# A graph layer's last two token blocks, computed as a fifth pair in seven products instead of eight

## The chip, the cores and the metric

The kernel runs on one core of one Trainium2 chip. The metric is the device time of one execution in microseconds (us); the time before is the median of three runs, 1125.27 us (1124.78 to 1126.44). The engines are named as in the profile: PE multiplies matrices (PEld is its loading of the stationary operand), DVE is the vector engine, ACT the scalar engine, POOL the GpSimd engine, and SP only issues DMAs here.

## The reference

`x` holds 1250 tokens (graph nodes) of width D = 1024; `src` and `dst` name 40000 edges. Two graph layers with a residual, then a mixture of eight experts with a residual:

```python
def _sage_layer(h, edge_src, edge_dst, deg_inv, W_self, W_neigh, b):
    msg = h[edge_src]
    agg = jax.ops.segment_sum(msg, edge_dst, num_segments=h.shape[0])
    mean = agg * deg_inv[:, None]
    return h @ W_self + mean @ W_neigh + b
...
deg_inv = 1.0 / jnp.maximum(deg, 1.0)
h = jax.nn.relu(_sage_layer(x, edge_src, edge_dst, deg_inv, W_self0, W_neigh0, b0))
out = _sage_layer(h, edge_src, edge_dst, deg_inv, W_self1, W_neigh1, b1)
...
x = x + _L0_gnn_ref(_layernorm(x, axis=-1), src, dst, ...)
x = x + _L0_ffn_ref(_layernorm(x, axis=-1)[None], ...)[0]
```

All is float32. `_L0_ffn_ref` routes each token to two of eight experts by a two-layer router (`rw1`, `rw2`) and adds their weighted outputs.

## The kernel before

**Blocks.** The tokens lie in NB = 10 blocks of P = 128; block 9 has 98. `hT1` holds the first layer's output transposed: 8 slices of 128 features (KD = 8) by 1250 tokens. `C` holds, for every pair of blocks, how often each source is joined to each target, so a sum over edges is a product with `C`.

**First layer.** It goes by four quarters q of the columns: products of the tokens with `w_neigh0` (`y_unit`, L514), then products with `C` (L550), whose sums DVE multiplies by `dinv` (1/degree along the free axis, made at q = 0, L543 and L544), adds to `hT1` (L557, L558), and ACT passes through a relu (L559). Temporary rows lie in `tmp`, a stretch of the scratch area `SC`.

**Second layer.** It works in column halves of 512, four in all: two of `w_neigh1` (`y_half`, each followed by `sum_half`, the product with `C`) and two of `w_self1` (`own_half`). Within a half, blocks 0 to 7 are taken as four pairs (j, 4+j) by `two_blocks`. The two blocks (as columns B), the two halves of the features and the two column quarters of the weights (A) make a product of two 2x2 block matrices, and it is done in seven block products of KB = 4 matmuls instead of eight (the Strassen-Winograd scheme). For that, DVE makes sums of tokens once (`T1`, `T2`, `T4` in `ts`, and `T3` over the second half's tokens in `hT1`) and sums of weights in every half (`S1` to `S4`, `weight_sums`). The order of the products on PE is A11, S2, A12, S3, S1, A22, S4 (L628); ACT copies the first to `u2` (L636), DVE adds further products to `u2` and `u3`, and `store` hands on four quarters of rows. Each of `u2`, `u3` and the `spare` rows of `store` lies in a ring in `SC`. Blocks 8 and 9, which no pair holds, are multiplied plainly by `plain_rows`: 8 matmuls of 512 columns each (L615).

**Where the plain blocks stand.** They come first in both `y_half` calls and in `own_half` 0, and last in `own_half` 1. `y_half` splits every result into a high and a low part (`zh` by ACT at L382, `zl` by DVE at L383). `sum_half` loads `x` for a block into a ring of six buffers `xs` in `SC` (L693, SP's queue), POOL adds `b1` (L694), PE multiplies `C` with `zh` and `zl` (L698), DVE multiplies by `dinv_p` (1/degree by partition) and adds (L702), and SP stores the rows to `v_d` (L703). `dinv_p` is made by 20 DVE instructions at the head of the second layer (L607, L608), from `dinv`.

**Own halves and the end.** `xa` is loaded from `v_d` (L724), and `own_half` adds the products to it: DVE where a quarter is ready in PSUM (L140, the line of the helper `tt` that records every DVE tensor operation), POOL otherwise (L744). The weight sums of the last half are made between the two own halves. In the last half `finish` runs for each finished block: layernorm on DVE (L319 to L326, a root on ACT at L323), a store to `t_d`, POOL's `xa += t` (L340), the store to `out` (L341); two blocks later `turn_back` transposes the normalised rows on PE (L774) and ACT copies them into `hT1` (L778). Then the router begins: its `token_sums` on DVE write `xw`, which lies over `xa`, so they wait for the last store from `xa`; PE meanwhile has other products (L1174, L1188, L1127).

**Order.** The order of instructions on each engine is set when the program is built, by a scheduler that takes what its model says is ready; on the chip each engine goes strictly in that order, and so does each DMA queue. PSUM tiles go round in pools: `mm` (3 tiles, name `ps`), `mmb` (3, name `psb`), `tpp` (2, name `tp`, for transposes).

Of the kernel before, what the change touches and what calls it, by code (L numbers as in the profile page):

```python
# [10 lines left out]
F32 = mybir.dt.float32  # L11
# [3 lines left out]
I32 = mybir.dt.int32  # L15
# [6 lines left out]
P = 128  # L22
# [7 lines left out]
def kernel(  # L30
# [165 lines left out]
    nc.scalar.dma_start(out=b0_p, in_=b0.rearrange("(k p) -> p k", p=P))  # L196


    ext = const.tile([R, 3, 2], F32, name="ext")
    base_i = const.tile([1, NGR], I32, name="base_i")  # L200

    keys = const.tile([GP, 2, 2 * GC, R], F32, name="keys")
    worst = const.tile([1, 1], F32, name="worst")
    plain = const.tile([1, 1], I32, name="plain")
    gx = L[:1, 8000 : 8000 + 3 * NGR].rearrange("o (a g) -> o a g", a=3)
# [138 lines left out]
    def gnn_windows():  # L344
# [28 lines left out]

        yh = yp.tile([P, NB, QW], F32R, name="yh")
        yl = yp.tile([P, NB, QW], F32R, name="yl")
        win = yp.tile([P, NB * WIN], F16, name="win")
        win_i = yp.tile([P, NB * WIN], I32, name="win_i")
        nc.gpsimd.iota(win_i, pattern=[[1, NB * WIN]], base=0, channel_multiplier=0)
# [143 lines left out]
        for q in range(4):  # L522
            w_q = w_next
            w_next = load_q(w_neigh0, q + 1) if q < 3 else None
            for b in range(NB):
                if q == 0:
                    some_groups(1)
                y_unit(w_q, h0T, b, yh[: rows[b], b, :], yl[: rows[b], b, :])
            if q == 3:
                w_half = load_half(w_neigh1, 0)  # L530
            if q == 0:
                some_groups(R)
                while open_rows:
                    close_row()

                for c0, n in cchunks:
                    ps = mm.tile([P, 512], F32, name="ps")
                    for k in range(NB):
                        nc.tensor.matmul(
                            ps[:, :n], ones_r, C[:, k, c0 : c0 + n],  # L540
                            start=(k == 0), stop=(k == NB - 1),
                        )
                    nc.vector.tensor_scalar(dinv[:, c0 : c0 + n], ps[:, :n], 1.0, None, op0=ALU.max)  # L543
                    nc.vector.reciprocal(dinv[:, c0 : c0 + n], dinv[:, c0 : c0 + n])  # L544
            for c0, n in cchunks:
                for d in (2 * q, 2 * q + 1):
                    ps = mm.tile([P, 512], F32, name="ps")
                    for k in range(NB):
                        for part in (yh, yl):
                            nc.tensor.matmul(  # L550
                                ps[:, :n], part[: rows[k], k, (d % 2) * P : (d % 2 + 1) * P],
                                C[: rows[k], k, c0 : c0 + n],
                                start=(k == 0 and part is yh), stop=(k == NB - 1 and part is yl),
                            )
                    t = tmp[:, n_tmp % 4, :n]
                    n_tmp += 1
                    nc.vector.tensor_tensor(t, ps[:, :n], dinv[:, c0 : c0 + n], ALU.mult)  # L557
                    nc.vector.tensor_tensor(t, t, hT1[:, d, c0 : c0 + n], ALU.add)  # L558
                    nc.scalar.activation(hT1[:, d, c0 : c0 + n], t, AF.Relu)  # L559
        y0.close()  # L560


# [37 lines left out]
                tt(B12[:, i, :], B22[:, i, :], B12[:, i, :], ALU.subtract)  # L600
        T3 = B12

        dinv_p = small.tile([P, NB], F32, name="dinv_p")
        for b in range(NB):
            m = rows[b]
            d_t = tmp[:, b % 4, :P]
            nc.vector.tensor_tensor(d_t[:m, :m], dinv[:m, blk(b)], ident[:m, :m], ALU.mult)  # L607
            nc.vector.tensor_reduce(dinv_p[:m, b : b + 1], d_t[:m, :m], AX.X, ALU.add)  # L608
        nc.sync.dma_start(out=row_of(3), in_=bcast(b1, D))

        def plain_rows(w, b):
            m = rows[b]
            ps = mm.tile([P, 512], F32, name="ps")
            for k in range(KD):
                nc.tensor.matmul(  # L615
                    ps[:m], hT1[:, k, blk(b)], w[:, k, :], start=(k == 0), stop=(k == KD - 1)
                )
            return ps[:m]

        def two_blocks(ws, j, u, store):  # L620

            A11, A12, A22, S1, S2, S3, S4 = ws
            b, b2 = j, NA + j
            js = slice(j * P, (j + 1) * P)

            def product(ps, rows_of, w, first):
                for k in range(KB):
                    nc.tensor.matmul(  # L628
                        ps, rows_of(k), w[:, k, :], start=(first and k == 0),
                        stop=(k == KB - 1), skip_group_check=not first,  # L630
                    )

            u2, u3 = u[:, 0, :], u[:, 1, :]
            pa = mm.tile([P, 512], F32, name="ps")[:, :QW]
            product(pa, lambda k: hT1[:, k, blk(b)], A11, True)
            nc.scalar.copy(u2, pa)  # L636
            pb = mm.tile([P, 512], F32, name="ps")[:, :QW]
            product(pb, lambda k: T2[:, k, js], S2, True)
            tt(u2, u2, pb, ALU.add)
            product(pa, lambda k: hT1[:, KB + k, blk(b)], A12, False)  # L640
            store(b, 0, pa, None)
            pc = mmb.tile([P, 512], F32, name="psb")[:, :QW]
            product(pc, lambda k: T3[:, k, js], S3, True)
            tt(u3, u2, pc, ALU.add)
            pd = mmb.tile([P, 512], F32, name="psb")[:, :QW]
            product(pd, lambda k: T1[:, k, js], S1, True)
            store(b2, 1, pd, u3)
            product(pc, lambda k: T4[:, k, js], A22, False)
            store(b, 1, pc, u2)
            product(pd, lambda k: hT1[:, KB + k, blk(b2)], S4, False)  # L650
            store(b2, 0, pd, u2)

        def ring(v, n):
            v = v.rearrange("p (a n) -> p a n", n=QW)
# [7 lines left out]

        us, _ = ring(SC[:, :1024], 4)
        _, spare = ring(SC[:, 1024:2048], 4)
        xs = SC[:, : 3 * D].rearrange("p (a n) -> p a n", n=HALF)
        b1_r = row_of(3)

        with tc.tile_pool(name="y1", bufs=1, side="right") as y1:
            yh = y1.tile([P, NB, HALF], F32R, name="zh")
            yl = y1.tile([P, NB, HALF], F32R, name="zl")  # L670

            def y_half(ws):
                for b in range(2 * NA, NB):
                    split(yh[: rows[b], b, :], yl[: rows[b], b, :], plain_rows(w_half, b))

                def store(b, c, ps, u):
                    if u is not None:
                        t = spare()
                        tt(t, u, ps, ALU.add)
                        ps = t  # L680
                    cs = slice(c * QW, (c + 1) * QW)
                    split(yh[:, b, cs], yl[:, b, cs], ps)

                for j in range(NA):
                    two_blocks(ws, j, us[:, 2 * (j % 2) : 2 * (j % 2) + 2, :], store)

            def sum_half(h):

                hs = slice(h * HALF, (h + 1) * HALF)
                for b in range(NB):  # L690
                    m = rows[b]
                    v = xs[:m, 5 - b % 6, :]
                    nc.sync.dma_start(out=v, in_=x[blk(b), hs])  # L693
                    nc.gpsimd.tensor_tensor(v, v, b1_r[:m, hs], ALU.add)  # L694
                    ps = mm.tile([P, 512], F32, name="ps")
# [6 lines left out]
                    stt(v, ps[:m], dinv_p[:m, b : b + 1], v, op0=ALU.mult, op1=ALU.add)  # L702
                    nc.sync.dma_start(out=v_d[blk(b), hs], in_=v)  # L703

            y_half(ws)
            w_half = load_half(w_neigh1, 1)
            sum_half(0)
            ws = weight_sums(w_half, S_first)
            y_half(ws)
            w_half = load_half(w_self1, 0)  # L710
            sum_half(1)
            ws = weight_sums(w_half, S_first)
# [3 lines left out]
        own = st.enter_context(tc.tile_pool(name="own", bufs=1, side="right"))  # L716
        xa = own.tile([P, NB, D], F32, name="xa")
        more = own.tile([P, 2 * WQ + 4 * KB * QW + 2048], F32, name="more")
        alone = list(range(2 * NA, NB))
        paired = [b for j in range(NA) for b in (j, NA + j)]  # L720
        for h, order in enumerate((alone + paired, paired + alone)):
            hs = slice(h * HALF, (h + 1) * HALF)
            for b in order:
                nc.sync.dma_start(out=xa[: rows[b], b, hs], in_=v_d[blk(b), hs])  # L724
# [3 lines left out]
        _, spare = ring(more[:, -1024:], 4)  # L728

        def own_half(w, ws, h, done):  # L730
            def rows_alone():
                for b in alone:
                    v = xa[: rows[b], b, h * HALF : (h + 1) * HALF]
                    tt(v, v, plain_rows(w, b), ALU.add)
                    done(b)

            def store(b, c, ps, u):
                v = xa[:, b, h * HALF + c * QW : h * HALF + (c + 1) * QW]
                if u is None:
                    tt(v, v, ps, ALU.add)  # L740
                else:
                    t = spare()
                    tt(t, u, ps, ALU.add)
                    nc.gpsimd.tensor_tensor(v, v, t, ALU.add)  # L744

            if h == 0:
                rows_alone()
            for j in range(NA):
                two_blocks(ws, j, us[:, 2 * (j % 2) : 2 * (j % 2) + 2, :], store)
                done(j)  # L750
                done(NA + j)
            if h == 1:
                rows_alone()

        n_done = [0]

        def finish(b):
            t = row_of(n_done[0] % 4)
            n_done[0] += 1
            after_layers(b, xa, t)  # L760
            turned.append((b, t))
# [5 lines left out]
        def turn_back():  # L767
# [3 lines left out]
            for q in range(0, KD, 4):  # L771
# [5 lines left out]
                for i in range(4):  # L777
                    nc.scalar.copy(hT1[:, q + i, blk(b)], ps[:, i, :m])  # L778

        own_half(w_half, ws, 0, lambda b: None)  # L780
        ws = weight_sums(w_last, more[:, 2 * WQ : -2048])
        turn[0] = 0
        route_w.append(load_pair(rw1, 0))
        route_w.append(load_pair(rw1, 1))
        own_half(w_last, ws, 1, finish)
        while turned:
            turn_back()
        st.close()
# [919 lines left out]
```

## Time and profile before

| what | us |
|---|---|
| median of the three runs | 1125.27 |
| time of the profiled execution | 1124.47 |
| span of its profile | 1122.5 |
| PE busy | 1090.3 |
| plain blocks of one half, L615 (433.41 to 447.15) | 13.74 |
| one pair of one half, 7 products, L628 (447.15 to 459.23) | 12.08 |
| `sum_half`, L698 (495.66 to 542.11 on the chain) | 46.45 |
| the ten sums for `dinv_p`, L607 and L608, each mean | 0.287 and 0.284 |

The profile is of one execution; times in it count from the start of its span. A float32 matmul of the program shows as two MATMUL records. "Busy" of PE is modelled, since matmuls are pipelined: the distance between the starts of two records is the better measure, and the table's stage times are such distances.

### The profile page before, as it was taken

What the parts mean: (1) busy time and instruction counts of PE and PEld (TensorE: products, weight loads), DVE (VectorE), ACT (ScalarE), POOL (GpSimd) and SP (SyncE); (2) the same over time, 40 slices, a digit from 0 to 9 for tenths busy, and PEclk for the clock granted to TensorE, in tenths of its full rate; (3) what the DMA queues carried; (4) which work ended last, traced back from release to release, by engine and by line L of the source; (5) the groups of instructions that cost most, each with busy time, mean ns of one, the idle gap of its engine ahead of it and who ended that gap; (6) DMA issues with size and microseconds to landing.
All of it is one profiled execution on the core that took longest, in us unless ns stands there. A gap on an engine that the chain in (4) does not pass through costs nothing.

```text
span 1122.5 us, 13221 instructions
## 1 busy us (share of the span) xinstructions
PE 1090.3 (97%) x4729; PEld 786.5 (70%) x4729; DVE 466.2 (42%) x1145; ACT 185.3 (17%) x418; POOL 334.6 (30%) x441
## 2 busy tenths in 40 slices
PE   6999999999999999999999999999999999999994
PEld 5555556888888886888688868886544487676762
DVE  8777777762121236233134122364522173222221
ACT  4301000001111111110011000022211134232321
POOL 2899999900000000013002202254000013332321
PEclk9999999999999999999999999999999999999997
DMA  7011011010100021032103270334870456767763
GB/s 239 31 38 40 1 38 39 1 38 1 38 1 1 1 75 38 1 125 98 36 1 131 92 273 3 90 158 166 313 240 1 149 184 171 185 181 194 194 169 51
DMA packets 62317, 107.33 MB, mean 96 GB/s; under 512 B 8906, under 2 KB 35690, under 8 KB 62240
## 3 DMA queue, kind: packets, MB, share of 16 engines
q1 hardware_dynamic: 51392, 79.69, 20.8%
q0 software_dynamic: 7056, 23.88, 9.1%
q10 hardware_dynamic: 3792, 2.79, 0.8%
q8 instruction: 42, 0.69, 0.3%
q14 instruction: 35, 0.29, 0.1%
HBM read 80.74 MB, written 27.42 MB: 96 GB/s over the span
## 4 chain that ended last, share of the span: by engine, by line
PE 91%; DMA 3%; POOL 2%; DVE 2%; issue 1%; ACT 0%; SPq 0%; DVEq 0%; POOLq 0%
PE ps L514 12%; PE ps L451 11%; PE psb L628 10%; PE ps L698 8%; PE ps L550 8%; PE ps L628 7%; PE ps L1519 6%; PE ps L1546 6%; PE ps L1174 5%; PE ps L615 5%; PE ps L1188 4%; PE cnt L412 3%; DMA out_dram<-L 2%; PE ps L1127 2%; POOL ol L402 1%; PE tp L1502 1%
## 5 line engine op out<-in xcount | busy, mean ns | idle before, releaser
L402 POOL TENSOR_SCALAR ol<-lane,keys 125x128 f16<-125x128 f16 x320 | 192.8, 621 | 23.6 <-DVE oh L409 23.6
L451 PE MATMUL ps<-h0T,L 128*128 128x498 f32 (+2 forms) x384 | 147.9, 517 | 0.6 <-DMA L<-in_L_gnn_W_self_dram 0.4
L694 POOL TENSOR_TENSOR L<-L 128x512 f32<-128x512 f32 (+1 forms) x20 | 31.7, 1595 | 374.0 <-DMA L<-in_L_gnn_b_dram 215.3
L514 PE MATMUL ps<-L,h0T 128*128 128x256 f32 (+1 forms) x640 | 142.0, 379 | 0.0
L514 PEld LDWEIGHTS ps<-L,h0T 128*128 128x128 f32 (+1 forms) x640 | 118.4, 188 | 17.9 <-issue 0.5
L409 DVE TENSOR_SCALAR oh<-win,keys 125x240 f16<-125x240 f16 x320 | 83.6, 315 | 32.0 <-PE cnt L412 29.8
L451 PEld LDWEIGHTS ps<-h0T,L 128*128 128x128 f32 x384 | 67.5, 191 | 38.5 <-issue 34.0
L1519 PE MATMUL ps<-xw,L 128*128 x368 | 84.1, 380 | 0.7 <-issue 0.7
L1546 PE MATMUL ps<-xw,L 128*128 x184 | 82.8, 593 | 0.5 <-ACT L L1534 0.5
L550 PE MATMUL ps<-C,yh 128*128 128x256 f32 (+2 forms) x240 | 81.8, 356 | 0.0
L550 PE MATMUL ps<-C,yl 128*128 128x256 f32 (+2 forms) x240 | 81.5, 353 | 0.0
L698 PE MATMUL ps<-zh,C 128*128 128x512 f32 (+1 forms) x200 | 79.5, 398 | 0.0
L698 PE MATMUL ps<-zl,C 128*128 128x512 f32 (+1 forms) x200 | 78.6, 393 | 0.0
L1519 PEld LDWEIGHTS ps<-xw,L 128*128 128x128 f32 x368 | 68.0, 190 | 9.6 <-issue 1.4
L1552 POOL DMA_INDIRECT out_dram<-L x23 | 36.5, 1586 | 118.4 <-DVE L L1551 85.7
L431 DVE TENSOR_TENSOR C<-C,cnt 128x240 f32 x160 | 64.3, 402 | 11.7 <-DVE C L431 1.0
L1491 POOL DMA_INDIRECT L<-t_d,L x26 | 25.5, 979 | 143.9 <-DVE L L140 123.1
L1546 PEld LDWEIGHTS ps<-xw,L 128*128 128x128 f32 x184 | 34.9, 190 | 34.9 <-issue 32.3
L412 PEld LDWEIGHTS <-ol 125*128 125x128 f16 x320 | 31.0, 97 | 37.0 <-POOL ol L402 22.1
L1551 DVE SCALAR_TENSOR_TENSOR L<-ps,L 128x512 f32<-128x512 f32 x46 | 34.5, 751 | 53.1 <-PE ps L1546 53.1
L383 DVE TENSOR_TENSOR yl<-ps,yh 128x256 fp32r<-128x256 f32 (+1 forms) x40 | 16.9, 424 | 92.5 <-ACT yh L382 92.5
L140 DVE TENSOR_TENSOR L<-L,ps 128x512 f32<-128x512 f32 (+1 forms) x28 | 17.1, 611 | 86.7 <-PE ps L1174 44.5
(223 smaller groups left out, 1523.4 us busy)
## 6 DMA issues: line engine op xcount, KB each, us to landing
xw<-in_L_ffn_ew_dram SPq DMA_DIRECT2D x16, 1024.0 KB, 10.6
L<-in_L_ffn_eb_dram SPq DMA_DIRECT2D x23, 512.0 KB, 4.0
L<-in_x_dram SPq DMA_DIRECT2D x20, 256.0 KB, 2.8
v_d<-L SPq DMA_DIRECT2D x18, 256.0 KB, 2.0
xa<-v_d SPq DMA_DIRECT2D x18, 256.0 KB, 6.2
t_d<-L SPq DMA_DIRECT2D x9, 512.0 KB, 3.2
out_dram<-xa SPq DMA_DIRECT2D x9, 512.0 KB, 2.7
L<-in_L_gnn_W_self_dram SPq DMA_DIRECT2D x4, 1024.0 KB, 5.5
```

The lines of the kernel that those rows point to most:

```text
L402: nc.gpsimd.tensor_scalar(ol[:, c, :], lane[:GP], keys[:, 1, c, r : r + 1], None, op0=ALU.is_equal)
L409: nc.vector.tensor_scalar(oh, win[:GP], keys[:, 0, i * GC + c, r : r + 1], None, op0=ALU.is_equal)
L412: nc.tensor.matmul(ps[:, i, :GW], ol[:, i * GC + c, :], oh, start=(c == 0), stop=(c == GC - 1),)
L431: nc.vector.tensor_tensor(to, to.bitcast(F32), ps[:, i, :GW].rearrange("p (k w) -> p k w", k=NB), ALU.add,)
L451: nc.tensor.matmul(ps[:, :n], w[:, k, (d % 2) * P : (d % 2 + 1) * P], h0T[:, k, c0 : c0 + n], start=(k == 0), stop=(k == KD - 1),)
L514: nc.tensor.matmul(ps[:m, :QW], hT[:, k, blk(b)], w[:, k, :], start=(k == 0), stop=(k == KD - 1))
L550: nc.tensor.matmul(ps[:, :n], part[: rows[k], k, (d % 2) * P : (d % 2 + 1) * P], C[: rows[k], k, c0 : c0 + n], start=(k == 0 and part is y ...
L615: nc.tensor.matmul(ps[:m], hT1[:, k, blk(b)], w[:, k, :], start=(k == 0), stop=(k == KD - 1))
L628: nc.tensor.matmul(ps, rows_of(k), w[:, k, :], start=(first and k == 0), stop=(k == KB - 1), skip_group_check=not first,)
L698: nc.tensor.matmul(ps[:m], C[: rows[k], k, blk(b)], part[: rows[k], k, :], start=(k == 0 and part is yh), stop=(k == NB - 1 and part is yl),)
L1519: nc.tensor.matmul(ps[:, :H], xT[:, k, :], w1_all[:, ds(e, 1), k * H : (k + 1) * H], start=(k == 0), stop=(k == KD - 1),)
L1546: nc.tensor.matmul(ps, hT[:, q, :], w2_all[:, ds(e, 1), q * D + h * HALF : q * D + (h + 1) * HALF], start=(q == 0), stop=(q == KH - 1),)
```

## The change

In the second layer, blocks 8 and 9 become a fifth pair of `two_blocks` in all four halves, and `plain_rows` is gone. Their token sums `Te1`, `Te3` lie in a new tile `te`, `Te2`, `Te4` in `SC` (elements 2048 to 3071), made once by `last_sums`: five DVE instructions and one ACT copy. Since block 9 has 98 rows, its products have 98 output rows, the last rows of `u3` are copied from `u2` by ACT, and the A22 product goes to a PSUM tile of its own (`pe`).

What goes with it: the first two pairs of `y_half` 0 start with their A11 and A12 products (`amid`), ahead of all that use the token sums. `dinv_p` is made in the first layer at q = 0. The ring `xs` has four buffers, which lie over the rings of `u2`, `u3` and `spare`. `xa` is loaded in the order of the pairs, blocks 8 and 9 last. The last half's weight sums are made inside `own_half` 0, after its second pair. `finish` uses three row buffers in turn, not four. `ext`, `base_i` and `keys` move to the pool of the first layer.

```diff
+            if q == 0:
+                dinv_p = small.tile([P, NB], F32, name="dinv_p")
+                for b in range(NB):
+                    m = rows[b]
+                    d_t = tmp[:, b % 4, :P]
+                    nc.vector.tensor_tensor(d_t[:m, :m], dinv[:m, blk(b)], ident[:m, :m], ALU.mult)
+                    nc.vector.tensor_reduce(dinv_p[:m, b : b + 1], d_t[:m, :m], AX.X, ALU.add)
...
+        def last_sums():
+            B11, B21 = hT1[:, :KB, blk(b8)], hT1[:, KB:, blk(b8)]
+            B12, B22 = hT1[:, :KB, blk(b9)], hT1[:, KB:, blk(b9)]
+            tt(Te1, B12, B11[:, :, :M2], ALU.subtract)
+            tt(Te2[:, :, :M2], B22, Te1, ALU.subtract)
+            nc.scalar.copy(Te2[:, :, M2:], B11[:, :, M2:])
+            tt(Te4, B21, Te2, ALU.subtract)
+            tt(Te3, B22, B12, ALU.subtract)
...
-        def plain_rows(w, b):
-            m = rows[b]
-            ps = mm.tile([P, 512], F32, name="ps")
-            for k in range(KD):
-                nc.tensor.matmul(
-                    ps[:m], hT1[:, k, blk(b)], w[:, k, :], start=(k == 0), stop=(k == KD - 1)
-                )
-            return ps[:m]
...
             product(pa, lambda k: hT1[:, k, blk(b)], A11, True)
             nc.scalar.copy(u2, pa)
+            yield
+            if amid:
+                product(pa, lambda k: hT1[:, KB + k, blk(b)], A12, False)
+                store(b, 0, pa, None)
+                yield
...
+            product(pc[:m2], lambda k: t3[:, k, :], S3, True)
+            if m2 < P:
+                past = slice(m2 // LQ * LQ, P)
+                nc.scalar.copy(u3[past], u2[past])
+            tt(u3[:m2], u2[:m2], pc[:m2], ALU.add)
...
+            if m2 == P:
+                product(pc, lambda k: t4[:, k, :], A22, False)
+                store(b, 1, pc, u2)
+            else:
+                pe = mmb.tile([P, 512], F32, name="psb")[:, :QW]
+                product(pe, lambda k: t4[:, k, :], A22, True)
+                store(b, 1, pe, u3)
...
-            def y_half(ws):
-                for b in range(2 * NA, NB):
-                    split(yh[: rows[b], b, :], yl[: rows[b], b, :], plain_rows(w_half, b))
...
+                if h == 0:
+                    two = [pair(j, True) for j in range(2)]
+                    for _ in range(2):
+                        for p in two:
+                            next(p)
+                    for p in two:
+                        list(p)
+                for j in range(0 if h else 2, NA + 1):
+                    list(pair(j))
...
-                    v = xs[:m, 5 - b % 6, :]
+                    v = xs[:m, 3 - b % 4, :]
...
+            for j in range(NA + 1):
+                list(two_blocks(ws, j, us[:, 2 * (j % 2) : 2 * (j % 2) + 2, :], store))
+                if h == 0 and j == 1:
+                    ws_last.extend(weight_sums(w_last, more[:, 2 * WQ : -2048]))
+                for b in (j, NA + j) if j < NA else (b8, b9):
+                    done(b)
...
-            t = row_of(n_done[0] % 4)
+            t = row_of((0, 1, 3)[n_done[0] % 3])
```

## The prediction

> **What bounds the kernel now.** I read the page's first, second and fourth part, then the groups by line and shape, then the timeline at the places where the change puts an edge. First the page:
>
> ```profile
> PE 1090.3 (97%) x4729; PEld 786.5 (70%) x4729; DVE 466.2 (42%) x1145; ACT 185.3 (17%) x418; POOL 334.6 (30%) x441
> ...
> PE   6999999999999999999999999999999999999994
> ...
> PEclk9999999999999999999999999999999999999997
> ...
> PE 91%; DMA 3%; POOL 2%; DVE 2%; issue 1%; ACT 0%; SPq 0%; DVEq 0%; POOLq 0%
> ```
>
> PE is busy in every slice at an undivided clock, and the chain that ended last runs through PE for 91%. From 433 to 782 us, the second layer, no other engine stands on the chain. So what PE saves there comes off the end, unless a new wait takes it. The groups by line and shape, L615 the plain blocks and L628 the products of pairs:
>
> ```profile
> L615 PE MATMUL ps<-L 128*128 128x512 f32 x48 | 21.1, 592 | 0.0
> L615 PE MATMUL ps<-L 128*98 128x512 f32 x48 | 21.1, 592 | 0.0
> ...
> L628 PE MATMUL ps<-L 128*128 128x256 f32 x192 | 45.4, 379 | 0.0
> ```
>
> The reader sees no idle time ahead of either, and that 98 output rows cost as much as 128: the moving columns set the time. Distances of starts, from the timeline of PE:
>
> ```profile
> 433.41 13.90 PE L615 MATMUL ps<-L 128*128 128x512 f32 x32
> 447.15 1.89 PE L628 MATMUL ps<-L 128*128 128x256 f32 x8
> 448.87 1.89 PE L628 MATMUL ps<-ts 128*128 128x256 f32 x8
> ...
> 459.23 1.89 PE L628 MATMUL ps<-L 128*128 128x256 f32 x8
> ```
>
> Last, the edge from the layer to the router, all engines; E below is the end of the last half's products, 781.96 here:
>
> ```profile
> 781.96 1.04 PE L774 MATMUL tp<-ident,L 128*128 128x128 f32 x8
> 782.60 1.45 ACT L778 COPY L<-tp 128x128 f32<-128x128 f32 x8 [6.11 <-PE tp L774]
> 783.86 0.37 ACT L323 ACTIVATE rs<-mv,eps 98x1 f32<-98x1 f32 x1
> 784.51 1.45 ACT L778 COPY L<-tp 128x128 f32<-128x128 f32 x8 [0.28 <-PE tp L774]
> 785.35 2.37 POOL L340 TENSOR_TENSOR xa<-xa,L 98x1024 f32<-98x1024 f32 x1 [5.39 <-DVE L L326]
> 787.75 0.35 SPq L341 DMA_DIRECT2D out_dram<-xa  x1
> 788.15 0.92 PE L1127 MATMUL ps<-L 128*128 128x226 f32 x4
> 791.00 2.89 DVE L140 TENSOR_TENSOR xw<-L 128x2048 f32<-128x2048 f32 x2 [5.74 <-DMA out_dram<-xa]
> 798.00 2.31 PE L1174 MATMUL ps<-xw 128*128 128x512 f32 x5
> ```
>
> Here block 9's finish, its store and the router's token sums run beside PE's transposes and first products. The sums (T2 and S2, done by 796.7) are in time for 798.00 with 1.3 us to spare.
>
> **Part 1, the products.** Removed in each half: 2 blocks, 32 records, 447.15 - 433.41 = 13.74 us. Added: 7 products of 8 records, 459.23 - 447.15 = 12.08 us; the 98-row ones count the same by the two L615 rows. Saved: 1.66 us a half, 6.64 us in four halves. All of it lies on the path.
>
> The row of 256 columns (12.08/56 = 215.7 ns a record) costs half of the row of 512 (13.74/32 = 429.4 ns). The Trainium skill, in "TensorE: Matmul & The Clock Gate", section "Back-to-back issue gap", adds a fixed 2.5 ns to every stream of columns, and "Perfetto Trace Analysis", section "Matmuls", says that "Larger matmuls are more efficient than smaller matmuls, when possible"; both speak against cutting 512 into 256. By the page, at two streams of 109.2 and 215.8 ns to a record, an estimate, the saving would be 4 x (13.81 - 12.23) = 6.3 us. The rows show no such penalty.
>
> **Part 2, the end of the last half.** Before, blocks 8 and 9 finished 7.7 us apart (774.22 and 781.96), with PE at work in between. Now both finish at E, as blocks 1 and 5 do at 751.05, and that end gives the rows. There the sixth product ends at 749.32; DVE adds at 749.52, POOL at 750.03, statistics run at 750.78. So block 8's statistics stand at E - 0.3, its root on ACT at E + 0.7, its normalising (L326, 1.25) to E + 2.6; block 9's statistics (0.69) and aggregate (0.21) to E + 3.4, root to E + 3.75, normalising to E + 5.5 (1.64, the L326 row beside POOL's L340 at 769.83).
>
> The order of the changed program on ACT is: root of 8, copies of block 3, root of 9, copies of 7 and 8, copies of 9. Before, the copies of 7 stood ahead of the last root. Eight copies take 1.45 us and `tp` has two tiles. So PE goes: transposes of 3 (E to 0.87), one router matmul (0.86), transposes of 7 behind the copies of 3 (to E + 3.0), one matmul (3.85); ACT is held at the root of 9 until E + 3.75, so 8's transposes run 4.6 to 5.7, a matmul to 6.6, 9's to 7.45, a matmul to 8.3. Then L1127. Before it stood at 788.15 - 781.96 = E + 6.2; with the transposes of block 3 (0.87), formerly ahead of E, 7.06 is work, and 8.3 - 7.06 = 1.24 us is new waiting. Transposes of 2 and 6 now fall among half-long matmuls, as at 736.76 to 740.69: 0.2 us more. Given back: 1.44 us. Bounds: nothing, if ACT's order does not bind; 3.6 if the last store from `xa` lands after 6.6 us (the slowest of the ten first `xa` loads) and not 3.15 (787.75 to 790.90). With 3.15, T2 and S2 come at E + 5.5 + 2.4 (L340) + 3.2 + 5.7 (791.00 to 796.7) = E + 16.8, and PE asks at 8.3 + 9.85 (788.15 to 798.00) = E + 18.15. With 6.6 PE waits 2.2 more. I take 1.44, since its rows are of the same operations.
>
> **Edits costed at nothing.**
> - `dinv_p`: 20 DVE instructions, 5.7 us, leave 426 to 440 us, where DVE had the slack, and enter the first quarter's L550 (238 to 261 us on PE). There DVE does 1.36 us of work for each 4.5 us of PE and idles some 3.1 us before every unit, so 2 to 3 sums (1.7 us) fit; without that cover the next splits would start up to 1.7 us late, under three PSUM tiles. No DMA moves with them.
> - Head of the layer: pairs 0 and 1 start with four products that need no sums (6.9 us, to 440.3). T2's last part ended about 436.9 and T4 at 438.7, both behind the last relu (435.65). `last_sums` stands behind them: about 0.56 x 4 (392 columns, between 0.42 at 256 and 0.69 at 512) + 0.69 = 2.9 us, to about 441.9 with a split between, and the first addition to `u2` is asked for at 442.0. A cover lost would cost that difference once.
> - `xs` of four, the queues: the first `x` of `sum_half` now waits for the last split, 1.6 us into it, and is issued behind the half's 2 MB of weights. The issue at 495.31 behind such weights took 7.3 us. SP's order still puts the weights ahead of it, at the row's 493.96. On DVE the sums S1 and S3 now stand ahead of the eviction of block 0 (L702), so that eviction waits for the weights: 502.0 + 3.46 + 0.75 = 506.2, 10.7 us into the stage; PE asks for that PSUM tile after three blocks, 3 x 4.65 = 13.9. Slack 3.2 us. At the other end of the rows, 12.1 us to land (the weights of the last half), PE waits 0.85 us in each of two halves: 0 to 1.7. A gain is excluded, since L698 has no idle before it.
> - `xa` in the order of pairs: DVE adds block 0 at 5.2 us into `own_half` 0, not at 18.9. The first load of that queue landed in 3.3 us, the slowest of ten in 6.6. If it took 10.5 (the slowest of twenty), DVE's `u3` would hold up the A22 product by about 3.1 us; else 0.
> - Sums of the last weights: same four instructions (1.22 each) inside a pair that comes after 668.1, where the weights landed; three row buffers: each is rewritten after its transposes in PE's order; POOL's extra adds (0.72 each) and ACT's copies of 32 rows end within a product.
>
> **Sum.** -6.64 + 1.44 = -5.20 us. The profiled execution, 1124.47 (span 1122.5), becomes 1119.27; it stood 0.80 under the median, so the median becomes 1120.1.
>
> **The rivals.**
> - A: the ACT order costs nothing, because the scheduler's gaps fall otherwise on the chip: -6.64, 1118.6. For it: at the earlier pair ends (736.76, 751.05) PE waited only 0.24 us for ACT. Against: two finishes at once.
> - B: the last store from `xa` decides, 2.2 us more: 1122.3. For it: the 5.74 us wait of DVE at 791.00 ends on that store. Against: slack 1.3.
> - C, mild and strong: the weights ahead of the eviction, at 12.1 us to land, 1.7 us more: 1121.8. It is also the case of the other side: the place is block 3 of `sum_half`, the price is 2 us per us of landing beyond 11.2, and from 14.9 us on the kernel is slower than before: 7.4 us of waiting eat the 5.2 and the bound of measurement, 1127.5. For it: the slowest expert load took 14.8. Against: such weights landed in 8.1 us at 502.0 and in 7.9 at 610.4.
> - D: the late `xa`, 3.1 us: 1123.2, no change. Against: block 0 is first in the queue.
>
> **How the numbers follow.** 0.2% (2.25 us) is about what a measurement of this kernel tells from no change. Chances: forecast 0.60, A 0.15, B 0.07, C mild 0.06, C strong 0.06, D 0.06. Faster holds all but D and strong C: 0.88; same 0.06; slower 0.06. The range takes in A with the spread of the runs below the median (0.5) and B: 1118.0 to 1122.4, leaving out D and strong C.
>
> **What would show it.** Right: no L615; L628 distances of 215 to 216 ns also where the form is 128*98; pairs of 12.1 us, five to a half; `sum_half` at 46.4 us with no idle; 6 to 9 us from the last product to L1127, with transposes waiting for L778. Wrong: PE waiting for L702 in `sum_half` (C), for `u3` in the first own pair (D), at the first product with `xw` (B), or products of the fifth pair that take longer than the others.

## The result and the profile after

The changed kernel takes 1122.63 us (median of 7 runs, 1120.86 to 1123.13), the kernel beside it 1125.85 (7 runs): a ratio of 0.9974, 95% interval 0.9965 to 0.9983, about 2.9 us faster. The forecast was 5.2 us faster; the sign was right, the size was not, and 1122.6 lies just outside the range. The profiled execution took 1122.76 us (span 1120.8), against 1124.47 (1122.5) before.

The page of the changed kernel, parts 1, 2 and 4 (busy time, PE's clock by slices, the chain that ended last):

```profile
PE 1084.8 (97%) x4825; PEld 803.8 (72%) x4825; DVE 473.7 (42%) x1171; ACT 189.2 (17%) x431; POOL 335.9 (30%) x447
...
PEclk9999999999999999999999999999999999999997
...
PE 75%; DMA 14%; DVE 4%; issue 4%; POOL 1%; ACT 1%; SPq 0%; POOLq 0%; DVEq 0%; ACTq 0%
```

PE is busy for 5.5 us less (before: 1090.3), and the span is only 1.7 us shorter: part of what was saved is idle now. Of the chain's 14% of DMA, 12% lies behind 942 us, in the experts' stores to `out`, which end beside PE's last products; an experiment below with the unchanged second layer shows the same 12% there. Whether a run's chain is followed through them says nothing about this change. Another 1% is the load of the last weights, which matters below.

PE's groups by line and form (L648 is the line of the pairs' products now; then busy time, mean ns of one, idle time before them and its cause):

```profile
L648 PE MATMUL ps<-L 128*128 128x256 f32 x240 | 56.2, 379 | 0.0
L648 PE MATMUL psb<-ts,L 128*128 128x256 f32 x192 | 45.5, 380 | 0.6 <-DVE more L140 0.6
L648 PE MATMUL psb<-L,ts 128*128 128x256 f32 x96 | 22.8, 380 | 0.6 <-DVE more L140 0.6
...
L648 PE MATMUL psb<-ts,te 128*98 128x256 f32 x48 | 10.8, 379 | 0.0
```

The plain blocks are gone, the 98-row products of the fifth pair cost the same 379 ns of modelled time, and two groups have idle time that no group of the pairs had before. PE's waits from 434 to 803 us, the second layer and the head of the router, say where (total, times, longest):

```profile
PE psb L648 <- DVE more L140: 1.2, 2, 0.6
PE ps L1214 <- DVE L L140: 0.9, 1, 0.9
PE tp L814 <- ACT L L818: 0.7, 3, 0.2
PE ps L1214 <- ACT L L818: 0.2, 1, 0.2
```

In the kernel before, the same view has one line, 0.5 us for ACT's copies. The waits for DVE, two in the pairs and one in the router's head, are new.

The stages, as distances of starts on PE (us; "half" is the first product of a column half to the first product after it):

| | before | after |
|---|---|---|
| `y_half` 0 | 61.90 | 60.25 |
| `sum_half` 0 | 46.64 | 46.66 |
| `y_half` 1 | 61.89 | 60.24 |
| `sum_half` 1 | 46.66 | 46.66 |
| `own_half` 0 | 62.08 | 62.17 |
| `own_half` 1, to the router's product S2 with T2 | 85.42 | 84.74 |
| from there to its product S3 with T3 | 4.50 | 5.56 |
| sum, layer's first product to the product with T3 | 369.09 | 366.28 |

The sum is 2.81 us shorter, close to the 2.9 of the result. Outside of it the two profiles differ by chance: the layer's first product stood at 433.41 us before and at 434.02 after, and between 432.2 and 434.0 in the eight further profiles below. So the sum of the table, not the span, is compared from here on.

**Where the first 1.7 us went.** The timeline of the first own half, its second pair (start, duration, engine, line, operation; in brackets the idle time before and what ended it). `more<-more 128x1024` are the four sums of the last weights:

```profile
654.22 0.38 SPq L133 DMA_DIRECT2D more<-in_L_gnn_W_self_dram  x1
...
665.09 1.89 PE L648 MATMUL psb<-ts,L 128*128 128x256 f32 x8
666.23 1.23 DVE L140 TENSOR_TENSOR more<-more 128x1024 f32<-128x1024 f32 x1 [1.80 <-DMA more<-in_L_gnn_W_self_dram]
666.82 1.89 PE L648 MATMUL psb<-ts 128*128 128x256 f32 x8
667.37 0.41 DVE L140 TENSOR_TENSOR xa<-xa,ps 128x256 f32<-128x256 f32 x1
667.70 1.22 DVE L140 TENSOR_TENSOR more<-more 128x1024 f32<-128x1024 f32 x1
668.84 0.42 DVE L140 TENSOR_TENSOR more<-more,psb 128x256 f32<-128x256 f32 x1
669.17 2.36 DVE L140 TENSOR_TENSOR more<-more 128x1024 f32<-128x1024 f32 x2
669.31 1.99 PE L648 MATMUL psb<-L,ts 128*128 128x256 f32 x8 [0.60 <-DVE more L140]
671.44 0.75 DVE L140 TENSOR_TENSOR more<-more,psb 128x256 f32<-128x256 f32 x2
671.91 1.99 PE L648 MATMUL psb<-ts,L 128*128 128x256 f32 x8 [0.61 <-DVE more L140]
673.74 1.89 PE L648 MATMUL ps<-L 128*128 128x256 f32 x8
```

The load of the last weights is issued at 654.22, behind the ten loads of `xa`'s first half, and lands at 666.23, 12.0 us later. DVE's order has the first of the four sums in the middle of the second pair, so DVE stands before it for 1.80 us, and the additions that empty PSUM for the next products come behind it. Products that lie 1.73 us apart elsewhere lie 2.49 (666.82 to 669.31), 2.60 and 1.83 us apart here: 0.76, 0.87 and 0.10 late, 1.73 us together. It is as much as the fifth pair was to save in this half (1.66).

**Where a further 1.1 us went.** The end of the layer, PE, ACT, DVE and the last store. The last half's products end at 777.06 (E in the prediction):

```profile
777.06 1.04 PE L814 MATMUL tp<-ident,L 128*128 128x128 f32 x8
...
780.24 0.29 ACT L320 ACTIVATE rs<-mv,eps 98x1 f32<-98x1 f32 x1 [0.86 <-DVE mv L319]
780.83 1.59 DVE L323 TENSOR_SCALAR L<-xa,mv,rs 98x1024 f32<-98x1024 f32 x1
...
784.84 0.92 PE L1167 MATMUL ps<-L 128*128 128x226 f32 x4
784.94 0.35 SPq L338 DMA_DIRECT2D out_dram<-xa  x1
788.94 2.89 DVE L140 TENSOR_TENSOR xw<-L 128x2048 f32<-128x2048 f32 x2 [6.52 <-DMA out_dram<-xa]
...
793.95 0.69 DVE L140 TENSOR_TENSOR xw<-xw,L 128x512 f32<-128x512 f32 x1
794.55 2.29 DVE L140 TENSOR_TENSOR xw<-L,xw 128x2048 f32<-128x2048 f32 x1
794.74 3.67 PE L1214 MATMUL ps<-xw 128*128 128x512 f32 x8
797.96 2.28 DVE L140 TENSOR_TENSOR L<-L 128x2048 f32<-128x2048 f32 x1
800.30 3.70 PE L1214 MATMUL ps<-L,xw 128*128 128x512 f32 x8 [0.91 <-DVE L L140]
```

The last store from `xa` lands at 788.94, E + 11.9, and DVE's chain starts: T1, S1, T2, S2 (793.95), T4 (794.55), S3, S4, T3 (797.96). S2 ends at 794.64, only just for the product at 794.74: from the 28 records of L1167 to that product it is 5.47 us, against 5.34 before, so 0.13 us is lost there. T3, the next that PE asks for, is late by more: 0.91 us. Before, T3 was done at 802.31 and its product started at 802.50 without a wait:

```profile
800.03 2.28 DVE L140 TENSOR_TENSOR L<-L 128x2048 f32<-128x2048 f32 x1
...
802.50 3.70 PE L1174 MATMUL ps<-L,xw 128*128 128x512 f32 x8
```

### The profile page after: what moved, and what is told of

It reads as the page before. It is cut to its first block, busy times and chain, and to the rows that moved or that the text cites. A ratio compares the mean times of both kernels' runs of the same rounds, so it can differ in the third digit from the quotient of the medians.

```text
span 1120.8 us, 13458 instructions
## 1 busy us (share of the span) xinstructions
PE 1084.8 (97%) x4825; PEld 803.8 (72%) x4825; DVE 473.7 (42%) x1171; ACT 189.2 (17%) x431; POOL 335.9 (30%) x447
## 4 chain that ended last, share of the span: by engine, by line
PE 75%; DMA 14%; DVE 4%; issue 4%; POOL 1%; ACT 1%; SPq 0%; POOLq 0%; DVEq 0%; ACTq 0%
PE ps L516 12%; DMA out_dram<-L 12%; PE ps L453 12%; PE psb L648 11%; PE ps L744 8%; PE ps L648 8%; PE ps L552 8%; PE ps L1214 4%; PE ps L1228 3%; PE cnt L414 3%; PE ps L1167 1%; DMA more<-in_L_gnn_W_self_dram 1%; DVE xw L140 1%; DVE L L140 1%; PE tp L306 1%
## 5 line engine op out<-in xcount | busy, mean ns | idle before, releaser
L740 POOL TENSOR_TENSOR L<-L 128x512 f32<-128x512 f32 (+1 forms) x20 | 27.7, 1394 | 383.4 <-DMA L<-in_x_dram 383.4
L648 PE MATMUL ps<-L 128*128 128x256 f32 x240 | 56.2, 379 | 0.0
```

Source lines behind the costliest of these rows:

```text
L648: nc.tensor.matmul(ps, rows_of(k), w[:, k, :], start=(first and k == 0), stop=(k == KB - 1), skip_group_check=not first,)
```

## The experiments

Theory W: the missing gain is (1) the last weights, which land inside a pair whose additions stand behind their sums on DVE, and (2) T3, which stands behind T4 in a chain that starts with the last store. Each edit is made to the changed kernel if nothing else is said. The intervals of the ratios are some 0.0012 (1.3 us) to each side, so the sizes are read from the stages; the ratios say whether they arrive.

### The sums of the last weights behind the pair

```diff
-            tt(S1, A21, A22, ALU.add)
+            pin(nc.vector.tensor_tensor(S1, A21, A22, ALU.add))
...
-            tt(S3, A11, A21, ALU.subtract)
+            pin(nc.vector.tensor_tensor(S3, A11, A21, ALU.subtract))
...
-                    ws_last.extend(weight_sums(w_last, more[:, 2 * WQ : -2048]))
+                    ws_last.extend(weight_sums(w_last, more[:, 2 * WQ : -2048], tc.keep_in_program_order))
```

> The four sums of the last weights are issued on DVE behind the last addition of the second pair of the first own half, not in its middle. Theory W (late weights): in the changed kernel these weights landed at 666.23 us, in the middle of the second pair, and DVE stood before them while PE needed its additions; behind the pair (from about 672.5 us) they are there, no product of this half waits, the half takes 5 x 12.09 = 60.4 us instead of 62.16, and the kernel is 1.7 us shorter than the changed one (about 0.9959 of the kernel before, against 0.9974). Rival R1 (DVE's own work): the four sums, 4.9 us of DVE, hold up a pair wherever they stand; the wait moves into the third pair, the half stays at 61.5 to 62.2 us and the ratio at 0.997.

Measured: 1120.57 us (5 runs) against 1125.5, ratio 0.9945, 0.9932 to 0.9958, wholly below that of the changed kernel. The half takes 60.44 us, 1.73 less. The sums stand in the third pair now (L596 and L598 are those that the edit ties behind all that the program has put on DVE by then):

```profile
671.46 1.22 DVE L596 TENSOR_TENSOR more<-more 128x1024 f32<-128x1024 f32 x1
672.52 1.89 PE L648 MATMUL ps<-ts 128*128 128x256 f32 x8
672.71 1.64 DVE L140 TENSOR_TENSOR more<-more 128x1024 f32<-128x1024 f32 x1
...
675.98 1.89 PE L648 MATMUL psb<-ts,L 128*128 128x256 f32 x8
676.54 0.41 DVE L140 TENSOR_TENSOR more<-more,ps 128x256 f32<-128x256 f32 x1
```

All four in a row hold up an addition of that pair until 676.54, and PE goes on at its distance of 1.73 us. R1 falls, and (1) holds: it is not DVE's work.

### The last weights ahead of `xa` in the queue

```diff
+            if h == 0:
+                w_last = load_half(w_self1, 1, more[:, : 2 * WQ])
             for b in order:
                 nc.sync.dma_start(out=xa[: rows[b], b, hs], in_=v_d[blk(b), hs])
-            if h == 0:
-                w_last = load_half(w_self1, 1, more[:, : 2 * WQ])
...
+            with tc.issue_after(behind) if behind else nullcontext():
                 tt(S1, A21, A22, ALU.add)
```

`behind` is the addition to `xa` of the second pair; the sums are issued behind it, one addition later than in the changed kernel, and so stay in that pair.

> The load of the last weights is issued ahead of the ten loads of xa, some 6 us earlier; the sums stay in the second pair (all four behind the addition of xa there). W: the weights land near 660.2 us, before the sums are due (665), and the half takes 60.4 to 60.6 us: 1.6 to 1.7 us less than the changed kernel. R1: the sums are where they were, so the half stays at about 62.2 us. Rival D of the prediction (late xa): the first blocks of xa now share the DMA engines with 2 MB of weights; the first addition to xa (at 653.2 us before) comes late and the first pair waits up to 3 us, so that nothing is gained or the kernel is up to 1.5 us slower than the changed one.

Measured: 1119.96 us, ratio 0.9946, 0.9934 to 0.9959; the half takes 60.43 us.

```profile
647.73 0.38 SPq L133 DMA_DIRECT2D more<-in_L_gnn_W_self_dram  x1
...
657.07 0.42 DVE L782 TENSOR_TENSOR xa<-xa,ps 128x256 f32<-128x256 f32 x1 [0.32 <-DMA xa<-v_d]
...
665.30 2.35 DVE L140 TENSOR_TENSOR more<-more 128x1024 f32<-128x1024 f32 x2
666.49 1.89 PE L649 MATMUL psb<-ts 128*128 128x256 f32 x8
...
668.22 1.89 PE L649 MATMUL psb<-L,ts 128*128 128x256 f32 x8
```

The same sums in the same pair, and PE waits for nothing: at the head of the queue the weights took 8.1 us from issue to landing, not 12. The late `xa` shows too: the first block came at 657.07, 9.6 us into the half (5.4 in the changed kernel), and cost nothing, because in this kernel's order the pair's additions to `u2` and `u3` stand ahead of it. Rival D was real in its cause and free in its effect here.

The four kernels that left the sums as they were give the size a second way. How late the first sum started (us into the half), and the length of the half: 18.26 and 62.03 (plain end, below), 18.40 and 62.17 (changed kernel), 18.76 and 62.53 (T4 behind T3), 18.86 and 62.63 (copies first). Every hundredth of lateness is a hundredth of the half; by the same line, a half of 60.43 stands for 16.66 us (an estimate), and whatever lands before that should be free.

### Blocks 8 and 9 plain in the last half

```diff
-            for j in range(NA + 1):
+            for j in range(NA + 1 - h):
...
+            if h == 1:
+                for b in (b8, b9):
+                    v = xa[: rows[b], b, HALF:]
+                    tt(v, v, plain_rows(w, b), ALU.add)
+                    done(b)
```

> Only in the last own half, blocks 8 and 9 are computed plainly at the end, as in the kernel before; the other three halves keep the fifth pair. The prediction's terms: the fifth pair saves 1.66 us there and gives back 1.44, so this kernel is 0.2 us slower than the changed one. Theory W, from the two traces (last own half to the first product with xw's third sum: 89.83 us before, 90.14 after): the fifth pair gives back 1.97 us there, 0.5 for ACT's order, 0.9 for the third token sum, the rest in smaller steps; this kernel is 0.3 us faster than the changed one. In both, the first product with the third token sum waits for nothing (802.50 us before).

Measured: 1121.99 us (12 runs), ratio 0.9970, 0.9958 to 0.9982: no difference from the changed kernel that a run can tell. By the stages, `own_half` 1 takes 85.33 + 4.73 = 90.06 us to the product with T3, against 84.74 + 5.56 = 90.30: the fifth pair of the last half loses 0.24 us where the prediction had it gain 0.22. But the last store took 3.50 us here and 4.00 there, a larger difference than the 0.24, so this pair of runs doesn't settle the sign. The product with T3 waits 0.15 us here, where both forecasts had no wait.

### T4 behind T3

```diff
             tt(T2, B22, T1, ALU.subtract)
-            tt(T4, B21, T2, ALU.subtract)
...
             tt(T3, B22, B12, ALU.subtract)
+            tt(T4, B21, T2, ALU.subtract)
```

> In the router's token sums T4 is computed behind T3 on DVE instead of ahead of it. W: the 0.91 us in which PE stood before the first product with T3 (800.30 us) is DVE's chain from the last store of xa (landed 788.9) through T1, S1, T2, S2, T4, S3, S4 to T3; with T4 (2.29 us) out of it T3 is done at about 797.9 us, PE starts at 799.4 and the kernel is 0.9 us shorter than the changed one. Rival: the additions to u2 and u3, which now stand behind T4, come late and hold up the next products by about as much, or the time given back is lost at the experts anyway: no difference.

Measured: 1121.18 us, ratio 0.9960, 0.9946 to 0.9973; better than the changed kernel's 0.9974, but the intervals overlap. The stage shows it:

```profile
788.23 2.89 DVE L140 TENSOR_TENSOR xw<-L 128x2048 f32<-128x2048 f32 x2 [6.49 <-DMA out_dram<-xa]
...
795.05 2.28 DVE L140 TENSOR_TENSOR L<-L 128x2048 f32<-128x2048 f32 x1
797.25 2.28 DVE L140 TENSOR_TENSOR xw<-L,xw 128x2048 f32<-128x2048 f32 x1
...
798.61 3.70 PE L1214 MATMUL ps<-L,xw 128*128 128x512 f32 x8
```

T3 starts 6.8 us behind the landing instead of 9.0, its product waits no more, and the stretch from the product with T2 takes 4.58 us, 0.98 less. The additions behind T4 (799.46) hold up nothing. In this execution 0.4 us of it went to a longer wait for the weights, and 0.67 to a later landing of the first gather of tokens (PE waited 1.08 us for it at 916 us, 0.41 in the changed kernel, none in five of the ten profiles); both are landing times of other transfers.

### The same edit in the kernel before

T4 behind T3 in the kernel before, nothing else.

> The kernel before, with T4 behind T3 in the router's token sums, and nothing else. W: there the first product with T3 started at 802.50 without a wait (T3 done at 802.2), so the order of the sums is worth nothing before the change: ratio 1.000 within 0.0013, and 369.1 us from the layer's first product to the product with T3. Rival (the order is a gain of its own, whatever the change): 0.9 us, ratio 0.9992 and 368.2 us.

Measured: 1125.29 us (12 runs) against 1125.05, ratio 1.0004, 0.9993 to 1.0015; 369.10 us for the sum of stages (369.09). T3 starts at 797.22 and its product at 801.93, 4.50 us behind the one with T2, as before. So T4's place costs only where the change made the chain late.

### ACT's copies ahead of the last root

```diff
-            after_layers(b, xa, t)
+            if b == b9:
+                turn_back()
+                with tc.issue_after(copied[-1]):
+                    after_layers(b, xa, t)
+            else:
+                after_layers(b, xa, t)
```

`copied` lists ACT's copies in `turn_back`; the root is issued behind the last of them.

> The changed kernel, and in its last pair ACT copies the transposes of block 7 ahead of the root for block 9 (the order that the kernel before had). Theory P (the term of the prediction: ACT's order costs 1.24 us): the transposes of blocks 7, 8 and 9 wait no longer, L1167's first product comes 0.5 to 0.7 us sooner after the end of the layer's products, and the kernel is 0.5 to 0.7 us faster. Theory W (DVE's chain from the last store decides, not ACT): the root of 9 comes 0.6 us later (780.85 for 780.24), and with it the normalising, the last store, T1 and T3; the first product with T3 starts 0.6 us later than 23.24 us after the end of the layer's products (777.06 to 800.30), and the kernel is 0.6 us slower.

Measured: 1121.20 us, ratio 0.9966, 0.9955 to 0.9978: no difference that a run can tell. The last half's products end at 776.86 here:

```profile
780.93 0.37 ACT L320 ACTIVATE rs<-mv,eps 98x1 f32<-98x1 f32 x1
...
781.59 0.81 DVE L323 TENSOR_SCALAR L<-xa,mv,rs 98x1024 f32<-98x1024 f32 x1
...
784.19 0.92 PE L1173 MATMUL ps<-L 128*128 128x226 f32 x4
784.93 0.35 SPq L338 DMA_DIRECT2D out_dram<-xa  x1
788.17 2.90 DVE L140 TENSOR_TENSOR xw<-L 128x2048 f32<-128x2048 f32 x2 [5.77 <-DMA out_dram<-xa]
...
799.53 3.70 PE L1220 MATMUL ps<-L,xw 128*128 128x512 f32 x8 [0.92 <-DVE L L140]
```

P has its first half: the products behind the transposes (L1173 here) start at E + 7.33, 0.45 us sooner than in the changed kernel (E + 7.78). But all of it is spent before T3, whose product waits 0.92 us again. W's size fell: the root is 0.9 us later against E, yet the store only 0.19 (E + 8.07 for 7.88), because the normalising took 0.81 us, not 1.59. In the changed kernel it began while POOL was still adding `xa` of block 8; here POOL was all but done. And the store landed in 3.24 us, not 4.00, or the product with T3 would have started at E + 23.43, 0.19 later than there, not at E + 22.67.

### Both mends, and both with the copies first

The weights ahead of `xa` and T4 behind T3; then the same with the copies first.

> Both mends together: the last weights are loaded ahead of xa (as in the run before with that edit, sums behind the addition of xa in the second pair), and T4 is computed behind T3. W: no wait for DVE is left in the own halves or at the first product with T3; from the first product of the layer (434.02 in the changed kernel) to that product (800.30) it takes 363.3 us, against 366.28 in the changed kernel and 363.79 with the weights alone (where that product still waited 0.4 us); median 1119.5 us, ratio 0.9943. If the two gains do not add, it stays at 363.8 and 0.9946.

> Both mends, and ACT's copies of block 7 ahead of the root for block 9. W: with T4 behind T3 the chain from the last store has 1.4 us to spare, so that the 0.6 us by which the last store comes later costs nothing and the 0.5 to 0.7 us of waiting for ACT's copies are gained: 362.7 us from the layer's first product to the first product with T3, median 1118.9 us. Otherwise (the store again late for T1 and T2, or PE's wait only moved to the next transposes): 363.3 us, as without the edit.

Measured: both mends 1119.03 us (1118.39 to 1119.42, 5 runs) against 1125.05, ratio 0.9946, 0.9934 to 0.9959; with the copies first 1119.52, 0.9953, 0.9940 to 0.9966. Of the waits for DVE in the second layer and the router's head none is left with both mends; the sum of stages is 363.33 us, as forecast, 5.76 less than before the change. With the copies first it is 363.56, and W's 362.7 is missed: PE comes sooner and then stands before S2, which has less to spare than T3 has with T4 behind it:

```profile
787.02 2.89 DVE L140 TENSOR_TENSOR xw<-L 128x2048 f32<-128x2048 f32 x2 [6.36 <-DMA out_dram<-xa]
...
792.82 3.67 PE L1221 MATMUL ps<-xw 128*128 128x512 f32 x8 [0.43 <-issue]
```

S2 had started on DVE at 792.03 and taken 0.69 us. So in these executions the chain from the last store bounds this end, and ACT's order gains nothing. What the order is worth by itself stays open: the store took 3.83 us here, and with the 3.24 of the run before it S2 would have been done some 0.6 us sooner (an estimate), ahead of PE. The kernel with both mends is faster than both kernels, before and changed; a run doesn't tell it from the mend of the weights alone (1119.96, 363.79).

## Why the prediction was wrong

**Right: the products.** -1.66 us a half was forecast, -1.65 measured in both `y_half`, and -1.64 in `own_half` 0 (62.08 to 60.44) once its wait was removed. The prediction set the rows against two rules of the Trainium skill ("TensorE: Matmul & The Clock Gate", section "Back-to-back issue gap", and "Perfetto Trace Analysis", section "Matmuls") and found no such penalty for the smaller matmuls in them. They show a small one: 215.7 ns for 256 columns is 1.0 ns more than half of 429.4. Without a penalty the four halves would save 4 x (13.74 - 28 x 0.4294) = 6.87 us; with the first page's fixed gap, which it gives for an isolated matmul, 6.3, an estimate; at the measured 1.65 a half it is 6.6, between the two. The forecast's 12.08 us for a pair held the penalty already, so it cost the prediction nothing.

**Wrong: "Sums of the last weights".** The step costed them at nothing, as "same four instructions (1.22 each) inside a pair that comes after 668.1, where the weights landed". The landing was taken from the old trace, the place from the text of the code, behind the second pair. The old trace had shown that the text doesn't give the place:

```profile
655.95 0.71 SPq L133 DMA_DIRECT2D more<-in_L_gnn_W_self_dram  x1
...
668.10 1.23 DVE L140 TENSOR_TENSOR more<-more 128x1024 f32<-128x1024 f32 x1 [2.97 <-DMA more<-in_L_gnn_W_self_dram]
```

There the text makes these sums between the two own halves, but DVE made them from 668.10 to 673.7, within the first pair (664.24 to 676.32) and 44 us ahead of the second own half; the weights landed 3.9 us into that pair, and PE waited for nothing. In DVE's order of the changed kernel the sums stand among that pair's additions; and the own halves begin 2.7 us earlier, for the very gain that was forecast, while the load's issue came only 1.7 us earlier. The weights landed 6.3 us into the second pair (659.91), and that cost 1.73 us. Two experiments, one with the sums later and one with the load earlier, recover all of it.

**Wrong: "in time for 798.00 with 1.3 us to spare".** The chain was read to T2 and S2 and no further. Its last link, T3, had 0.2 us to spare in the rows before, and by the prediction's own sum 0.25 in the changed kernel: done at E + 22.4 (16.8 and another 5.6, 796.70 to 802.31), asked for at E + 22.65 (18.15 and 4.50). Two sizes then went against it. The last store took 4.00 us, not 3.15, so T3 was done at E + 23.2; and PE was ready for it at E + 22.3, because ACT's order cost less than forecast. So the product with T3 came 1.06 us later behind the one with T2 than before. It is rival B's cause, the last store from `xa`, at another product and for half its price. The size hangs on that store. Three kernels share the changed kernel's order at this end: from the last half's first product to the product with T3 they took 90.30 us (changed kernel, store 4.00), 90.35 (sums behind the pair, 4.04) and 89.55 (weights ahead of `xa`, 3.27), against 89.92 (3.25) before. So with a quick store the last half gains 0.37 us, about the 0.22 forecast, and with a slow one it loses 0.4. The store took 3.72 us or more in five of the seven kernels that finish blocks 8 and 9 at once, and 3.25 to 3.50 in the three that do not; whether the change makes it slow or chance does is not shown.

**Mis-sized: ACT's order**, 1.24 us forecast. From E to L1167 it took 7.78 us; with 7.06 of work, as the prediction counts it, 0.72 was waiting. ACT was free of the root at 780.5, E + 3.5, not E + 3.75, and PE had matmuls between the transposes. The transposes among half-long matmuls, 0.2 forecast, cost about 0.4: from the half's first product to E the changed kernel took 67.06 us, of which 60.25 is five pairs, so six blocks' transposes took 6.81, 1.13 each; before, 69.38 less 61.9 is 7.48 for seven, 1.07 each. This takes nothing off the sum, since the block that no longer stands ahead of E had cost 1.07 there and not the 0.87 of the prediction: the stretch to E is 2.32 us shorter, and 1.66 + 0.87 - 0.2 = 2.33 was forecast.

Together: 5.20 - 1.73 - 1.06 + (1.24 - 0.72) - 0.05 (from L1167 to the product with T2, 9.90 us for 9.85) = 2.88, against 2.81 in the stages. The +0.52 and part of the -1.06 are one thing: what PE gained at ACT it waited for before T3.

**What was costed at nothing and was.** `dinv_p`: two or three of its sums stand in each of four idle stretches of DVE from 250 to 266 us, and no PE wait follows them. The head of the layer: `y_half` 0 with the new start takes 60.25 us, `y_half` 1 60.24. `xs` of four and the queue: 46.66 us in both `sum_half`, no wait. C's condition, weights that take 12.1 us, did not come: DVE's first sum of them starts 8.6 us behind their issue (492.98 to 501.56) in the first `sum_half` and 7.9 us behind it in the second; in the first, the first `x` is issued at 492.56, ahead of these weights and not behind them. `xa` by pairs: block 0's addition at 5.4 us, no wait (D). A (ACT's order for nothing) is out by the 0.72 us, and its time leaves out the waits for DVE. Of the 0.9 us of waits for ACT in four pieces, only one, 0.17 us, lies behind E; the other three are at pair ends as before (0.5 in two).

## What to carry to other kernels

When a change shortens the way to a transfer's consumer, work out the landing anew against the new start, and take the consumer's place from the engine's built order (a trace shows it), not from the lines of the program: an instruction that waits for a late load holds up everything behind it on its engine. When a chain on another engine feeds several products, give the slack of each link up to the last; the first link's slack says nothing about the third's. A late load is mended at either end, by its place in the queue or by the place of what consumes it.

## What was not expected of the hardware

- The same 2 MB of weights took 12.0 us to land behind ten 256 KB loads in the queue and 8.1 us ahead of them.
- The last normalising (98 x 1024 float32) took 1.59 us beside POOL's addition and 0.81 us when it began 0.96 us later against E, as POOL ended. The price beside POOL was in the prediction; that a later start loses almost nothing was not.
- One store of 98 rows to `out` took 3.24 to 4.04 us from issue to DVE's start behind it over ten profiles. Those 0.8 us, whose cause is not shown, are as large as the wait before T3, so the wait itself varies: 0.39 us where the store took 3.27, and 0.91 where it took 4.00 or 4.04, in kernels with the same order there.
